# Mixture of experts: a chunk's preparation given out piece by piece beside the first experts, and a second bank for the gates

## The chip, the cores and the metric

One core of one Trainium2 chip runs the kernel. The time is device microseconds of one execution. Lower is better. Six names are used for what works in parallel: PE is TensorE's matmul, PEld its weight load, DVE is VectorE, ACT is ScalarE, POOL is GpSimd, and SP is SyncE, which here only issues transfers.

## The reference

An activation `x` of 2048 tokens of 128 numbers goes through a chain of attention and feed-forward layers, each added to `x`. Five kinds of layer are used (the small linear Ffn0, Moe1, Mamba, Moe2, and Attn2, Attn3, Ffn3 at the end); the change is about the two mixtures of experts. Each of the two is applied twice:

```
x = x + 0.5 * _L1_ffn_ref(_layernorm(x, axis=-1), ...)      # Moe1
x = x + _L1_attn_ref(_layernorm(x, axis=-1), ...)           # Mamba
x = x + 0.5 * _L1_ffn_ref(_layernorm(x, axis=-1), ...)      # Moe1
x = x + 0.5 * _L2_ffn_ref(_layernorm(x, axis=-1), ...)      # Moe2
x = x + _L2_attn_ref(_layernorm(x, axis=-1), ...)           # Attn2
x = x + 0.5 * _L2_ffn_ref(_layernorm(x, axis=-1), ...)      # Moe2
```

Moe1 picks 2 of 16 experts for each token, and adds a shared expert:

```
logits = flat @ router_w.T
topk_scores, topk_idx = jax.lax.top_k(logits + router_bias, TOPK)
topk_scores = jax.nn.softmax(topk_scores, axis=-1)
combine = combine.at[jnp.arange(N)[:, None], topk_idx].add(topk_scores)
hidden = jax.nn.silu(gate_all) * up_all
down_all = jnp.einsum('nke,ked->nkd', hidden, down_proj)
out = jnp.einsum('nk,nkd->nd', combine, down_all)
sh_hidden = jax.nn.silu(flat @ sh_gate.T) * (flat @ sh_up.T)
```

Moe2 picks 4 of 16 experts. Each expert has a hidden layer of 256:

```
combine = jnp.sum(jax.nn.one_hot(topi, E, dtype=...) * topw[..., None], axis=2)
hmid = jax.nn.gelu(x @ w1e + b1e, approximate=False)
return (acc + (hmid @ w2e + b2e) * ce[:, None], None)
```

Both are computed densely: every expert works on every token, and the combination weight (zero for experts not picked) is multiplied in.

## The kernel before

`x` stays on the chip, transposed: 128 features on the partitions, 2048 tokens along the free axis. A stage (one layer) works on four chunks of 512 tokens. All matmuls of the experts are written three times, with the operands split into a high and a low half (`mm3`: high by high, high by low, low by high).

**An expert.** In Moe1 (`main`, L576) the main loop makes 9 steps: eight pairs of experts (each of hidden size 64, two side by side on 128 partitions) and the shared expert. A step computes gates `g` and ups `u` into PSUM, then `y = silu(g)` on ACT, `u = y * u` and `z = u * c` on DVE (the product with the combination weights), splits `z` into `yh` (ACT) and `yl` (POOL), and accumulates `o`. In the text a step of Moe1 is also called an expert. In Moe2 (`main`, L682) there are 16 experts of two half steps each: `h` into PSUM (four banks in turn), Gelu on ACT, the product with `c` on DVE (`h<-h,c` or `y<-h,c`, so 32 products in a chunk), the split (its low half on DVE or POOL), and `o`.

**The weights of the experts.** `c` is a tile with the combination weights of two steps, broadcast to all partitions. It comes by a transfer on SP from the DRAM tile `rows` (`group`, L518, transfer at L524); group 0 of a chunk serves the first two steps, group 1 the next two, and so on. Main asks for the next group at each even step. The pool of `c` has three buffers (`room`, L529), handed out in the order of the program.

**The preparation of a chunk.** It is a Python generator (`steps`) that the main loop of the chunk ahead of it is woven with, and it has five pieces: (1) the layer norm (`centred`, squares, a power on POOL, transposes), (2) the split of the normed tokens and the router's matmul to logits, (3) the choice of the top 2 or 4 with DVE reductions (`combine`, L446), (4) the softmax weights and the `comb` matrix, (5) its transposes on PE, the copy `row` on ACT, the transfer `rows<-row` on SP (L514), and behind it the transfer of the chunk's first group (`rows`, L507). That first group of the next chunk is called N0 below: in the program it stands between two groups of the chunk that is being worked on.

**The order.** `weave` (L328) drives the main generator; after its i-th step it gives out pieces of the other generator as long as the count `at` satisfies the line below. Other work joins in: splits of the next stage's weights and pieces of the next stage's own preparation (`joined`, `early`), each of which raises the total `prep` by its number.

```python
while not done and at * self.MAIN < i * prep:
```

`MAIN` is the number of steps, `PREP` the number that stands for the stage's own preparation, and `EARLY` how many pieces of the stage behind are taken in early. With MAIN, PREP of 9, 7 the five pieces come after steps 1, 2, 3, 4 and 6; with 16, 7 after steps 1, 3, 5, 7 and 10. Where other work joins, the places shift. A scheduler then orders each engine's instructions: the program's order is the priority, and an instruction of later pieces may be put ahead if it is thought ready earlier. The order on each engine is fixed when the kernel is built.

**PSUM.** It has eight banks of 128 x 512 floats. In Moe1 they are: two shared ones for preparation (`pp`), two lent in addition (`lend`, L266), one for `o`, one for `g`, two for `u`. In Moe2: two shared, one lent, one `o`, four `h`. `pt` hands out the shared and lent banks in turn.

**The last stage step of Attn2** (`run`, L1789) gives Moe2's weight splits and its first chunk's preparation beside its last block, with the total `after.PREP + k`, where k is the 16 splits.

Of the kernel before, what the change touches and what calls it, by code (L numbers as in the profile page):

```python
# [29 lines left out]
P = 128  # L30
NT = 2048
SEQ = 256
NB = 8
CH = 512
# [213 lines left out]
class Stage:  # L248
# [3 lines left out]
    EARLY = (0, 0)  # L252
# [27 lines left out]
    def enter(self):  # L280
        pass
# [4 lines left out]
    def run(self, st, then):  # L286
        for c in range(NCH):
            if c == NCH - 3:
                with self.m.behind():
                    after, gen = then()  # L290
            if c == NCH - 1:
                return self.weave(self.main(c, st), (after, gen))
            own, n, rest = self.steps(c + 1), 0, self.m.rest
            if c == NCH - 2 and after and after.todo:
                own, n = self.joined(own, after.splits(), len(after.todo))
                own, k = self.joined(own, gen, after.EARLY[1])
                st = self.weave(self.main(c, st), (self, own), self.PREP + n + k)
                continue
            if rest:
                own, n = self.joined(own, *rest)  # L300
            if c >= NCH - 3 and after:

                own, n = self.joined(own, gen, after.EARLY[c - NCH + 3])
            st = self.weave(self.main(c, st), (self, own), self.PREP + n)
            if rest:
                self.m.rest = self.m.under.close()
# [21 lines left out]
    def weave(self, main, ahead, prep=None):  # L328

        stage, gen = ahead  # L330
        res, done, at = None, gen is None, 0
        prep = prep or (stage.PREP if stage else 0)
        for i, _ in enumerate(main, 1):
            while not done and at * self.MAIN < i * prep:
                try:
                    next(gen)
                    at += 1
                except StopIteration as e:
                    res, done = e.value, True
        return res if done else stage.finish(gen)  # L340
# [36 lines left out]
class Ffn0(Stage):  # L377


    PIECES = 3  # L380
# [32 lines left out]
class Moe(Stage):  # L413

    RAW, LAG = 7, 2

    def split(self, w, src, share):


        n = src.shape[-1]  # L420
        self.raw = ExitStack()
        tp = self.m.tc.tile_pool(name="raw", bufs=self.RAW, side=self.side, reuse_waits="tile")
        self.todo = []
        pool = self.raw.enter_context(tp)
        for at in range(0, n, CH):
            k = slice(at, min(n, at + CH))
            lower = self.nc.gpsimd if at // CH % share < share - 1 else None
            self.todo.append((pool, w[0][:, k], w[1][:, k], src[:, k], lower))
        self.raws = [self.fetch(*x) for x in self.todo[: self.RAW]]
# [109 lines left out]
class Moe1(Moe):  # L539


    MAIN, PREP, EARLY = 9, 7, (1, 3)
    SIDE = 2

    def open(self, side):
# [24 lines left out]

    def enter(self):
        self.ps = self.pool("m1p", 1, late=True, space=PSUM)
        self.lend(2)
        self.yk = self.pool("m1y", 3, late=True)

    def main(self, c, st):  # L576
        m, ps, yk = self.m, self.ps, self.yk
        hh, hl, ct = st
        rows, cg = ct if ct[1] else self.given
        h = (hh[:], hl[:])  # L580

        part = lambda i, k: [w[:, (3 * k + i) * P : (3 * k + i + 1) * P] for w in self.w]
        op = self.t(ps, [P, CH], "o")
        for k in range(9):
            if k % 2 == 0 and k < 8:

                cs, cg = cg, k < 6 and self.group(rows, k // 2 + 1)
            g = self.t(ps, [P, CH], "g")
            m.mm3(g[:], part(1, k), h)
            u = self.t(ps, [P, CH], "u", bufs=2)  # L590
            m.mm3(u[:], part(0, k), h)
            y = self.t(yk, [P, CH], "y")
            m.act(y[:], g[:], AF.Silu)
            z = self.t(yk, [P, CH], "z")
            if k < 8:
                m.tt(u[:], y[:], u[:], ALU.mult)
                m.tt(z[:], u[:], cs[:, k % 2, :], ALU.mult)
            else:
                m.tt(z[:], y[:], u[:], ALU.mult)
            yh = self.t(yk, [P, CH], "yh", dtype=F32R)  # L600
            yl = self.t(yk, [P, CH], "yl", dtype=F32R)
            m.halves(yh[:], yl[:], z[:], self.nc.gpsimd)
            m.mm3(op[:], part(2, k), (yh[:], yl[:]), k == 0, k == 8)
            if k < 8:
                yield
        m.stt(m.x(c), op[:], 0.5, m.x(c), ALU.mult, ALU.add)
        yield


class Moe2(Moe):  # L610


    MAIN, PREP, EARLY = 16, 7, (0, 3)
    SIDE = 1

    def open(self, side):
# [179 lines left out]
class Attn0(Stage):  # L796


    MAIN, PREP = 17, 12
# [224 lines left out]
class Mamba(Stage):  # L1024


    MAIN, PREP, EARLY = 16, 26, (2, 10)
# [457 lines left out]
    def beside(self, main, gens):  # L1485

        for i, _ in enumerate(main):
            for k in self.PLAN[i]:
                if k in gens:
                    next(gens[k], None)  # L1490
            yield
        for gen in gens.values():
            for _ in gen:
                pass
# [48 lines left out]
class Attn2(Stage):  # L1543


    MAIN, PREP = 11, 30
# [232 lines left out]
    ps = None  # L1779
# [9 lines left out]
    def run(self, st, then):  # L1789
        ready, half = st  # L1790
        for s in range(NB - 2):
            ahead = self, self.mix(self.stack(s + 1, half), self.project(s + 2))
            ready, half = self.weave(self.main(s, ready), ahead)
        after, gen = then(False)
        n = after.EARLY[1] if after else 0
        main = self.main(NB - 2, ready)
        st = self.weave(main, (self, self.early(self.stack(NB - 1, half), gen, n)), 19 + n)
        self.more.close()
        if after is None:
            return self.weave(self.main(NB - 1, st), (after, gen))  # L1800
        after.load()
        k = len(after.todo)
        gen = self.early(gen, after.splits(), k)
        return self.weave(self.main(NB - 1, st), (after, gen), after.PREP + k)

    def main(self, s, st):
        m, nc, wk, ps = self.m, self.nc, self.mk, self.ps
# [61 lines left out]
class Attn3(Stage):  # L1869


    MAIN, PREP, EARLY = 5, 8, (4, 8)
# [468 lines left out]
```

## Time and profile before

| what | us |
|---|---|
| median of 3 runs | 2684.03 |
| the runs | 2673.51, 2684.03, 5309.02 |
| the profiled execution | 2682.87 |
| its span in the profile | 2681.1 |

The page's second part gives each engine's busy share in 40 slices of the span, in tenths, and the clock that was granted to TensorE:

```profile
PE   6999998978888998898986898997988799789997
DVE  3666555459999899999998667877876776457653
PEclk7999998989999899899887998999998899799998
```

A slice is 67 us. The first Moe1 lies in the 7th to 9th (411 to 551 us), Mamba behind it up to the 22nd, then the second Moe1 and the first Moe2 (1465 to 1809 us), Attn2, and the second Moe2 (2036 to 2277 us). In Mamba DVE and POOL set the pace, in the mixtures PE does. The page's fourth part follows the chain of work that ended last:

```profile
PE 44%; DVE 18%; DMA 11%; ACT 10%; POOL 7%; issue 6%; SPq 4%; DVEq 0%; ACTq 0%; POOLq 0%
```

Seen chunk by chunk, the windows in which the four chunks were worked on lasted 35, 32, 28 and 44 us in the first Moe1, 53 (with a load of weights at its start), 19, 30 and 15 in the second, 71, 54, 47 and 55 in the first Moe2, and 71, 70, 54 and 46 in the second.

Waits are read like this: `A <- B: 6.7, 8, 1.8` says that instructions of kind A waited for B for 6.7 us in all, 8 times, 1.8 us the longest. In a timeline the idle time ahead of an instruction stands in brackets at its end, with what ended it.

### The profile page before, as it was taken

What the parts mean: (1) busy time and instruction counts of PE and PEld (TensorE: products, weight loads), DVE (VectorE), ACT (ScalarE), POOL (GpSimd) and SP (SyncE); (2) the same over time, 40 slices, a digit from 0 to 9 for tenths busy, and PEclk for the clock granted to TensorE, in tenths of its full rate; (3) what the DMA queues carried; (4) which work ended last, traced back from release to release, by engine and by line L of the source; (5) the groups of instructions that cost most, each with busy time, mean ns of one, the idle gap of its engine ahead of it and who ended that gap; (6) DMA issues with size and microseconds to landing.
All of it is one profiled execution on the core that took longest, in us unless ns stands there. A gap on an engine that the chain in (4) does not pass through costs nothing.

```text
span 2681.1 us, 36786 instructions
## 1 busy us (share of the span) xinstructions
PE 2348.9 (88%) x11655; PEld 1463.9 (55%) x11655; DVE 1950.2 (73%) x3164; ACT 1884.1 (70%) x4390; POOL 1639.1 (61%) x1223
## 2 busy tenths in 40 slices
PE   6999998978888998898986898997988799789997
PEld 5777766643333333333322666776766677556655
DVE  3666555459999899999998667877876776457653
ACT  5877876677777777777654666784556687678875
POOL 2555555459999999999997854551125455434531
PEclk7999998989999899899887998999998899799998
DMA  6656653233443344333442442322223221244430
GB/s 167 136 129 142 142 122 99 66 89 88 115 94 79 84 91 114 80 81 76 93 101 61 117 122 97 103 68 64 67 68 108 83 78 58 60 82 91 96 60 9
DMA packets 136338, 246.53 MB, mean 92 GB/s; under 512 B 17008, under 2 KB 60976, under 8 KB 136144
## 3 DMA queue, kind: packets, MB, share of 16 engines
q1 hardware_dynamic: 134640, 240.45, 36.4%
q10 hardware_dynamic: 1248, 3.48, 0.6%
q8 instruction: 93, 1.52, 0.2%
q14 instruction: 101, 0.83, 0.1%
q0 software_dynamic: 256, 0.25, 0.0%
HBM read 138.11 MB, written 21.50 MB: 60 GB/s over the span
## 4 chain that ended last, share of the span: by engine, by line
PE 44%; DVE 18%; DMA 11%; ACT 10%; POOL 7%; issue 6%; SPq 4%; DVEq 0%; ACTq 0%; POOLq 0%
PE pp L135 12%; DVE hs L1344 8%; PE o L135 6%; PE h L135 5%; PE sp L135 4%; POOL hs L1350 4%; DVE up L143 4%; PE op L135 3%; DMA du<-du 3%; PE u L135 3%; PE ss L135 2%; PE y L135 2%; PE tp L999 2%; DMA c<-rows 2%; DMA kl<-kl 1%
## 5 line engine op out<-in xcount | busy, mean ns | idle before, releaser
L1350 POOL TENSOR_TENSOR hs<-hs,cl 128x1024 f32<-128x1024 f32 x256 | 602.5, 2372 | 67.2 <-DVE hs L1344 47.7
L1344 DVE TENSOR_TENSOR_SCAN hs<-dA,up 128x1024 f32<-128x1024 f32 x192 | 439.0, 2286 | 22.9
L135 PE MATMUL y<-hs,ysel 128*64 128x512 f32 x1024 | 302.5, 672 | 46.5 <-POOL hs L1350 44.4
L993 POOL TENSOR_SCALAR pr<-pr,sums 128x256 f32<-128x256 f32 x192 | 175.4, 924 | 187.1 <-DVE sums L988 171.1
L167 ACT ACTIVATE dA<-dt,negA 128x510 f32<-128x510 f32 x384 | 251.4, 713 | 5.8 <-DVE hs L1344 4.5
L143 DVE TENSOR_TENSOR up<-up,du 128x1024 f32<-128x1024 f32 x192 | 233.3, 1215 | 29.7 <-PE up L135 21.9
L167 ACT ACTIVATE h<-h,vec 128x512 f32<-128x512 f32 x256 | 168.1, 667 | 60.1 <-PE h L135 56.0
L227 POOL TENSOR_TENSOR ln_r<-ln_r,mhalf 128x2 f32<-128x2 f32 (+2 forms) x116 | 90.3, 779 | 185.2 <-ACT ln_r L167 183.6
L135 PE MATMUL pp<-xp,w_hi 128*128 128x512 f32 x320 | 139.9, 520 | 23.5 <-ACT pre L167 23.5
L201 POOL TENSOR_TENSOR yl<-y,yh 128x512 fp32r<-128x512 f32 x64 | 83.9, 1311 | 114.7 <-ACT yh L167 113.7
L1304 POOL TENSOR_TENSOR hs<-du,bl 128x1024 f32<-128x1024 f32 x64 | 151.8, 2372 | 0.0
L1344 DVE TENSOR_TENSOR_SCAN hs<-up,hs 128x1024 f32<-128x1024 f32 x64 | 145.1, 2268 | 2.9 <-POOL hs L1304 2.4
L135 PE MATMUL o<-yl,wh 128*128 128x512 f32 x328 | 137.2, 418 | 6.3 <-POOL yl L201 5.2
L135 PEld LDWEIGHTS y<-hs,ysel 128*64 128x64 f32 x1024 | 53.8, 143 | 162.7 <-POOL hs L1350 77.5
L201 POOL TENSOR_TENSOR yl<-z,yh 128x512 fp32r<-128x512 f32 x72 | 92.2, 1285 | 80.0 <-ACT yh L167 78.9
L135 PE MATMUL o<-yh,wh 128*128 128x512 f32 x328 | 135.2, 412 | 4.3 <-ACT yh L167 4.3
L167 ACT ACTIVATE pr<-sp,nmax 128x256 f32<-128x256 f32 x256 | 120.8, 483 | 23.2 <-DVE nmax L980 10.1
L135 PE MATMUL h<-hh,wh 128*128 128x512 f32 x256 | 107.3, 419 | 30.2 <-DVE y L143 29.1
L143 DVE TENSOR_TENSOR h<-h,c 128x512 f32<-128x512 f32 x128 | 89.0, 696 | 61.4 <-ACT h L167 40.1
L135 PE MATMUL up<-bp,bsel 128*128 128x512 f32 x192 | 101.8, 531 | 36.1 <-DVE hs L1344 31.7
L135 PE MATMUL o<-yh,wl 128*128 128x512 f32 x328 | 130.8, 399 | 0.0
L167 ACT ACTIVATE ln_q<-pp 128x128 f32<-128x128 f32 x348 | 97.0, 279 | 46.9 <-PE pp L135 38.9
(417 smaller groups left out, 6917.1 us busy)
## 6 DMA issues: line engine op xcount, KB each, us to landing
c<-rows SPq DMA_DIRECT2D x64, 512.0 KB
cl<-states SPq DMA_DIRECT2D x62, 512.0 KB
c<-rows SPq DMA_DIRECT2D x64, 256.0 KB
dt<-dt SPq DMA_DIRECT2D x128, 128.0 KB
du<-du SPq DMA_DIRECT2D x128, 128.0 KB
k<-kh SPq DMA_DIRECT2D x60, 256.0 KB
kl<-kl SPq DMA_DIRECT2D x60, 256.0 KB
scr<-hi SPq DMA_DIRECT2D x96, 128.0 KB
```

What stands on the lines that cost most here:

```text
L135: return self.pin(self.nc.tensor.matmul(out, lhsT, rhs, start=start, stop=stop))
L143: return self.pin(self.nc.vector.tensor_tensor(out, in0, in1, op))
L167: i = self.nc.scalar.activation(out, in_, func, **kw)
L201: i = (lower or self.nc.vector).tensor_tensor(lo, x, hi, ALU.subtract)
L227: self.nc.gpsimd.tensor_tensor(out, out, self.mhalf[:, 0 : out.shape[-1]], ALU.pow)
L993: nc.gpsimd.tensor_scalar(pr[:, t, :], pr[:, t, :], sums[:, t : t + 1], None, ALU.mult)
L999: nc.tensor.transpose(tp[:, j, t, :], pr[:, t, j * P : (j + 1) * P], m.ident[:])
L1304: self.m.pin(self.nc.gpsimd.tensor_tensor(self.hs[g][:], du[:], b, ALU.mult))
L1344: m.pin(nc.vector.tensor_tensor_scan(x[:].rearrange("p g t -> p (g t)"), self.decays.pop(g).rearrange("p g b t -> p (g b t)"), u[:].rearra ...
L1350: m.pin(nc.gpsimd.tensor_tensor(x[:], x[:], c, ALU.mult))
```

## The change

Four numbers change, and a name is added:

```diff
 class Moe(Stage):
     RAW, LAG = 7, 2
+    PIECES = 5
...
 class Moe1(Moe):
-    MAIN, PREP, EARLY = 9, 7, (1, 3)
+    MAIN, PREP, EARLY = 9, 9, (1, 3)
...
     def enter(self):
         self.ps = self.pool("m1p", 1, late=True, space=PSUM)
-        self.lend(2)
+        self.lend(1)
...
-            g = self.t(ps, [P, CH], "g")
+            g = self.t(ps, [P, CH], "g", bufs=2)
...
 class Moe2(Moe):
-    MAIN, PREP, EARLY = 16, 7, (0, 3)
+    MAIN, PREP, EARLY = 16, 16, (0, 3)
...
 Attn2.run
-        return self.weave(self.main(NB - 1, st), (after, gen), after.PREP + k)
+        return self.weave(self.main(NB - 1, st), (after, gen), after.PIECES + k)
```

With PREP equal to MAIN the five pieces come after steps 1, 2, 3, 4 and 5, one after each, in Moe1 as in Moe2. Where other work joins, the fifth piece comes after these steps (before, after): first Moe1, chunk 0: 7, 6; chunk 1: 7, 5; chunk 2: 5, 4; second Moe1, chunks 0 and 1: 6, 5; chunk 2: 4, 4; first Moe2, chunks 0 to 2: 10, 5; second Moe2: 10, 5; 12, 7; 9, 6. The last chunk of a stage takes the number of the stage behind it. In Moe1 the gates get a second PSUM bank, and preparation loses one of its four. In Attn2's last block the total is 21 where it was 23.

## The prediction

> **What bounds the kernel now.** I read the page's first part first, then the busy time of each engine in four stretches: the first Moe1 stage (411 to 551), the second Moe1 with the first Moe2 (1465 to 1582, 1582 to 1809) and the second Moe2 (2036 to 2277). They are 725 us of the 2681.1 us span; the change touches little else. Columns: the stretch, its length, then busy us of PE, PEld, DVE, ACT, POOL with instruction counts, granted PE clock, DMA share, GB/s.
>
> ```profile
> PE 2348.9 (88%) x11655; PEld 1463.9 (55%) x11655; DVE 1950.2 (73%) x3164; ACT 1884.1 (70%) x4390; POOL 1639.1 (61%) x1223
> ...
> 411.00:551.00 140.00, 126.73 (x518) 91.44 (x519) 67.98 (x152) 94.41 (x221) 73.10 (x64) 0.91 0.25 61
> 1465.00:1582.00 117.00, 98.39 (x424) 74.78 (x425) 71.71 (x186) 70.29 (x160) 80.44 (x66) 0.94 0.49 134
> 1582.00:1809.00 227.00, 210.58 (x939) 167.38 (x938) 172.52 (x379) 176.30 (x328) 120.08 (x120) 0.96 0.29 93
> 2036.00:2277.00 241.00, 218.07 (x980) 171.95 (x979) 171.97 (x365) 174.99 (x393) 123.07 (x112) 0.96 0.23 76
> ```
>
> PE is the busiest everywhere, idle 13.3, 18.6, 16.4 and 22.9 us: 71 us in all is the most that can be won, and 18.6 of it holds a load of weights. So I asked the second Moe2 who waits, and looked at the longest wait on SP, DVE and PE. First SP's timeline: start, us, queue, line, transfer, count.
>
> ```profile
> 2047.55 10.98 SPq L524 DMA_DIRECT2D c<-rows  x3
> 2081.91 0.32 SPq L514 DMA_DIRECT2D rows<-row  x1
> 2083.89 21.43 SPq L524 DMA_DIRECT2D c<-rows  x6
> ```
>
> ```profile
> SPq L514 <- ACT row L167: 57.6, 3, 23.4
> ```
>
> Then DVE and PE over the same microseconds.
>
> ```profile
> 2077.23 0.22 DVE L143 TENSOR_TENSOR comb<-comb,pp 128x64 f32<-128x64 f32 x1
> ...
> 2090.46 0.70 DVE L143 TENSOR_TENSOR h<-h,c 128x512 f32<-128x512 f32 x1 [10.51 <-DMA c<-rows]
> ```
>
> ```profile
> 2080.95 0.39 PE L135 MATMUL o<-yh,wl 128*128 128x512 f32 x1
> 2091.81 0.80 PE L135 MATMUL h<-hh,wh 128*128 128x512 f32 x1 [10.47 <-DVE y L143]
> 2092.40 0.63 PE L135 MATMUL h<-hl,wh 128*128 128x512 f32 x1
> ```
>
> The next chunk's selection ends (2077.45), its transposes and ACT copy follow, and `rows<-row` goes out at 2081.91, SP having waited 23.4 us for the copy. Only behind it come the next chunk's first group (N0) **and this chunk's own groups 6 and 7**: 24 products had been done (12 experts, groups 0 to 5), and product 25 waits until 2090.46. From `rows<-row` to that product it is 8.6 us, in the first Moe2 9.0 (1621.77 to 1630.73). So place on SP is what costs: whatever stands behind N0 waits for the whole preparation. The first Moe2 does the same, PE gap 8.1 us; chunk 1 of the second has a 5.5 us wait on DVE after product 28 and a PE gap of 3.4.
>
> What the rows wait for is a chain, not a place. First centred tile to rows: 1583.1 to 1621.8 = 39 us (first Moe2), 2038.4 to 2081.9 = 43 us (second). In the former the logits come near expert 6 though placed beside the third, the selection at 1599 to 1611, the combination at 1616 to 1619. In chunks 1 and 2 of the first Moe2 rows leave after 5 and 2 of the chunk's 32 products, ahead of a place beside expert 10: placement isn't binding there either.
>
> **The change, part by part.** All against the profiled execution, 2682.87 us (span 2681.1 plus 1.8), 1.2 under the median 2684.03; the runs spread from 2673.5.
>
> *Second bank for g.* No instruction is added. In Moe1's two stretches PE waits for its single bank:
>
> ```profile
> PE g L135 <- ACT y L167: 6.7, 8, 1.8
> PE u L135 <- DVE z L143: 5.8, 5, 2.6
> ```
>
> and 2.2 us in the first: 8.9 together. Next late is u's bank, freed by DVE: 5.8 and 3.5 us already. I give half of 8.9: **−4** (−8.9 to 0). A row of the skill speaks lower, in the page "TensorE: Matmul & The Clock Gate", section "HAM oscillation — how this bites in real kernels": in its thin-M kernel a double-buffered PSUM brought nothing further (126.6 to 125.5 us). By it this term would be nearly 0 and the sum 4 higher; no run here shows which.
>
> *One bank less for preparation* (lent 2 to 1, so 4 to 3 with the shared pair). Moe2 runs its preparation and the guests' projections on 3 already. In Moe1 the guests are Ffn0, Mamba and the weight splits. **+2**: near 0 since Moe2 lives with it; at most 8, some 16 Mamba and Ffn0 pieces at half a microsecond (the `pp` matmul's mean, 520 ns).
>
> *Pieces earlier in Moe1* (PREP 7 to 9): fifth piece from beside expert 6 or 7 to 5 or 4. Each piece carries its ACT, PE and POOL work, one `rows<-row` and two N0 transfers on SP. Two stalls of Moe1 lie behind rows: PE gaps of 1.6 (476.8) and 2.6 us (1556.7). Chains of 22 to 30 us fill most of a 19 to 35 us chunk whatever the place: **−1** (−4.2 to 0). In the first Moe1's chunk 2 N0 now also passes the own group 3: three experts more stand behind rows that came after its 9th product. **+1** (0 to 6.3: three experts at 19/9 = 2.1 us, from the second Moe1's shortest chunk); Mamba's pieces fill that hole (PE 28.0 of 28 us busy there now).
>
> *Moe2, PREP 7 to 16*: piece 5 moves from beside expert 10 to 5. SP takes N0 in program order, so groups 4 and 5 go behind it: what is ahead covers 8 experts, not 12. An undisturbed chunk (1707 to 1754, PE 46.94 of 47 us busy) is 47/16 = 2.93 us an expert: the cover loses 4 × 2.93 = 11.7 us. For it, DVE, on which the chain waits, is relieved of the four experts' work while the rows are being made: per expert two products (0.70 and 0.69) and an `yl` (0.68) = 2.07 us, together 8.3. Net 11.7 − 8.3 = +3.4 for each chunk where own groups now wait, with the clock's part below +4. If ACT or POOL and not DVE holds the chain, all 11.7 is paid; if precedence shortens it by more, the present stall (10.5) goes: −11 to +11.7, and I take the value near DVE because the combination's dozen DVE operations stand right behind products 23 and 24. First Moe2 chunk 0: **+4**. Second, chunk 0: **+4**, chunk 1 (place 12 to 7): **+3.4** (−3.4 to 11.7), chunk 2 (9 to 6): **+3** (0 to 11.7): its rows come when 10 experts are done, 12 being covered now and 8 then; 2 × 2.93 = 5.9 are missing, of which Attn3's pieces (PE 53.9 of 54 us there) fill half. First Moe2 chunks 1 and 2: rows are early, N0 only holds one of three c buffers longer. Two suffice: from 1704 on N0 held one, groups went out every 5.6 to 6.3 us, one lands in 3.7: 0.
>
> The clock: after gaps of 8.1 and 10.5 us matmuls start 0.43 us apart instead of 0.23, 12 and 8 of them: 2.4 and 1.6 us, already paid. The same page, section "What's actually happening", has an idle window of about 3.4 us halving the clock and as much busy time restoring it; the rows agree. By it a longer gap costs nothing more, a new one some 1.7 (an estimate).
>
> *Attn2's count* (7 + 16 to 5 + 16): pieces of its last block shift by one main step; **0** (−3 to 3, POOL's longest wait there is 4.4).
>
> *Next Moe2's pieces beside Moe1's last chunk* (PREP of the guest): 4 and 5 a step sooner, 0.
>
> Sum: −4 + 2 − 1 + 1 + 4 + 4 + 3.4 + 3 = **+12.4**, 2695 us.
>
> **The rivals.**
>
> R0, slower: the chain isn't relieved. It is latency over POOL's powers, PE's transposes and ACT, which the moved products don't touch. Then four Moe2 chunks pay 11.7 and Moe1 6.3, with the bank's 2: 46.8 + 6.3 + 2 = +55, **2738**. For it: the same 46 us for chunk 3's chain (1654 to 1700), which ran with nothing placed before it. It decides if the second Moe2's first chain still takes 43 us from the first centred tile to rows.
>
> R1, faster: the pieces move forward and rows with them. Gaps of 8.1 + 10.5 + 3.4 go, the slow clock's 4.0, the whole g 8.9 and Moe1's 4.2: −39.5, **2643**; at half of that 2663. For it: Moe1's chains are 22 to 30 us, and an early priority could give Moe2 the same; 8 experts cover 23 us. Against: the logits were three experts behind their place.
>
> R2, nothing: SP's order by readiness lets the groups pass N0, as in the first Moe2's chunks 1 and 2, and the bank is covered: **2683**. Against: 23.4 us of SP waiting in front of ready groups.
>
> **How the numbers follow.** Two per cent, 54 us, is about what a measurement here tells from no change: faster below 2630, slower above 2738. Forecast 0.50 (its own range 2683 to 2715), R0 0.15, R1 0.22, R2 0.13. The range leaves out the upper half of R0 and the lower third of R1: 2655 to 2738. R0 stands at the bound, so half of it, 0.08, and 0.04 of the forecast's tail are slower: 0.12. Of R1 0.04 is below 2630, if Moe1's holes go too. The rest, 0.84, is the same.
>
> **What would show it.** In the second Moe2's chunk 0, `rows<-row` with 16 products before it, not 24, and then a DVE wait for `c<-rows` at product 17 with a PE gap of 12 to 15 us behind it; the same in the first. That chain at 35 us instead of 43 shows the relief; 43 shows R0; 25 or less R1. In Moe1 `g <- ACT y` gone from PE's waits and `u <- DVE z` above 9.3 shows the bank's half. A wait of PE for a `pp` bank in Mamba's pieces would show the lent bank's price. It is wrong altogether if groups 4 and 5 go out ahead of rows.

## The result, and the profile after

The changed kernel takes 2712.4 us (median of 4 runs, 2705 to 2716) where the kernel before took 2678.8 beside it: a ratio of 1.0131, 95% interval [1.0089, 1.0173]. One execution of the kernel before took 5309 us; it is in its median, but not in the ratio, which compares fast runs alone. A later comparison on another chip gave 1.0097 [1.0070, 1.0124]. The change makes the kernel slower, clearly more than by chance, and by less than 2%. The forecast was 2695 with 2655 to 2738. Below, a gain or loss of a run in us is its ratio put on the time of the kernel before, so 35 and 26 us here.

The profiled execution has a span of 2703.4 us. These are its windows of the same stretches, cut at its own stage ends (the columns are those of before: stretch, length, busy us of PE, PEld, DVE, ACT and POOL, clock, DMA share, GB/s):

```profile
411.00:541.00 130.00, 116.66 (x513) 87.76 (x511) 68.18 (x149) 90.99 (x209) 71.18 (x62) 0.96 0.25 61
1463.00:1583.00 120.00, 99.98 (x429) 77.03 (x429) 74.84 (x181) 73.76 (x174) 81.69 (x68) 0.89 0.49 128
1583.00:1805.00 222.00, 207.67 (x910) 162.78 (x908) 167.69 (x370) 174.77 (x313) 119.40 (x119) 0.98 0.29 95
2040.50:2293.70 253.20, 224.86 (x971) 176.08 (x970) 169.39 (x364) 173.93 (x378) 122.76 (x111) 0.92 0.22 72
```

The first Moe2 (third line) is 222 us long instead of 227, the second 253 instead of 241, and PE has 28 us there in which it does nothing, and a granted clock of 0.92 instead of 0.96. The same microseconds as before, at the first rows of the second Moe2, on SP:

```profile
2052.08 0.33 SPq L525 DMA_DIRECT2D c<-rows  x1
2077.74 0.33 SPq L515 DMA_DIRECT2D rows<-row  x1
2079.36 33.68 SPq L525 DMA_DIRECT2D c<-rows  x8
```

on DVE:

```profile
2074.92 0.22 DVE L143 TENSOR_TENSOR comb<-comb,pp 128x64 f32<-128x64 f32 x1
...
2085.74 0.70 DVE L143 TENSOR_TENSOR h<-h,c 128x512 f32<-128x512 f32 x1 [9.97 <-DMA c<-rows]
```

and on PE:

```profile
2076.54 0.39 PE L135 MATMUL o<-yh,wl 128*128 128x512 f32 x1
2087.09 0.80 PE L135 MATMUL h<-hh,wh 128*128 128x512 f32 x1 [10.16 <-DVE y L143]
2087.68 0.63 PE L135 MATMUL h<-hl,wh 128*128 128x512 f32 x1
```

Before `rows<-row` only one group (group 3) goes out where three did; then SP issues nothing for 25 us. DVE has done 16 of the chunk's products, idles 9.97 us and PE 10.16 us. The third chunk, in which DVE had no wait for `c` before, has one now:

```profile
2218.48 0.70 DVE L143 TENSOR_TENSOR h<-h,c 128x512 f32<-128x512 f32 x1 [8.92 <-DMA c<-rows]
```

It is again product 17 of its chunk. Over the second Moe2, SP's wait for the copy grew from 57.6 to 83.1 us (three waits each):

```profile
SPq L515 <- ACT row L167: 83.1, 3, 34.1
```

Lengths of the stages by profile, in us, from the last addition to `x` of one stage to that of the next. Names with e_ are the experiments; two names in one row are two profiles of one kernel.

| kernel | Moe1 | Mamba | Moe1 | Moe2 | Attn2 | Moe2 | behind it |
|---|---|---|---|---|---|---|---|
| before | 141.7 | 916.9 | 115.9 | 226.8 | 227.3 | 240.4 | 404.6 |
| changed | 134.9 | 921.7 | 120.6 | 221.7 | 235.7 | 253.2 | 409.6 |
| changed, second profile (e_after) | 137.2 | 921.2 | 120.0 | 221.6 | 235.1 | 255.5 | 408.9 |
| e_a2: Attn2's total alone | 138.9 | 918.4 | 118.2 | 226.9 | 232.1 | 240.7 | 403.4 |
| e_bank: the banks alone | 136.1 | 921.5 | 121.4 | 214.4 | 232.7 | 234.1 | 414.1 |
| e_m1, e_m1again: Moe1's places alone | 141.7, 141.8 | 922.1, 914.1 | 120.1, 117.1 | 229.3, 229.3 | 231.4, 229.2 | 240.6, 240.8 | 415.2, 413.3 |
| e_m2: Moe2's places alone | 139.4 | 922.2 | 123.5 | 230.7 | 226.6 | 252.9 | 412.5 |
| e_mid: changed, N0 after step 10 | 134.9 | 925.0 | 118.6 | 216.0 | 234.8 | 234.1 | 412.0 |
| e_late: changed, N0 after step 13 | 136.9 | 928.2 | 119.4 | 211.2 | 230.9 | 220.9 | 416.2 |
| e_best: before, banks, Moe2's places, N0 after step 13 | 136.0 | 919.0 | 119.2 | 212.1 | 231.6 | 222.5 | 424.4 |
| e_late7: e_late, Moe1's places as before | 135.0 | 926.7 | 121.2 | 212.1 | 235.1 | 222.9 | 425.3 |
| e_bankm1: the banks and Moe1's places | 139.8 | 923.0 | 119.2 | 217.4 | 232.2 | 234.7 | 410.7 |
| e_jit: before, another order | 141.5 | 923.9 | 118.2 | 228.0 | 226.7 | 237.0 | 419.8 |

Before and e_a2 have the same program up to Attn2's last block, and nearly the same behind it. Their rows show what chance does: 3 us in the first Moe1, but 0.1 and 0.3 in the two Moe2. e_m2 has before's program up to the second Moe1, where Moe2's first pieces join, and its Mamba is 5 us longer: that too is chance. The two profiles of e_m1 differ by 8 us in Mamba and by 0.0 and 0.2 in Moe2. So the Moe2 columns can be read to a microsecond or two, Mamba's can't.

### The profile page after: what moved, and what is told of

Same layout as the page of the kernel before. It is cut to its first block, busy times and chain, and to the rows that moved or that the text cites. A ratio compares the mean times of both kernels' runs of the same rounds, so it can differ in the third digit from the quotient of the medians.

```text
span 2703.4 us, 36801 instructions
## 1 busy us (share of the span) xinstructions
PE 2351.0 (87%) x11655; PEld 1468.7 (54%) x11655; DVE 1959.1 (72%) x3164; ACT 1889.6 (70%) x4390; POOL 1640.3 (61%) x1223
## 4 chain that ended last, share of the span: by engine, by line
PE 35%; DVE 18%; DMA 8%; POOL 8%; ACT 8%; issue 5%; SPq 3%; DVEq 0%; POOLq 0%; ACTq 0%
PE pp L135 8%; DVE hs L1345 7%; PE o L135 7%; PE h L135 6%; POOL hs L1351 4%; DVE up L143 3%; PE u L135 3%; DMA du<-du 3%; PE sp L135 2%; PE ss L135 2%; PE y L135 1%; DMA c<-rows 1%; PE g L135 1%; POOL hs L1305 1%; PE acc L135 1%
## 5 line engine op out<-in xcount | busy, mean ns | idle before, releaser
L135 PE MATMUL o<-yl,wh 128*128 128x512 f32 x328 | 136.9, 418 | 9.0 <-POOL yl L201 4.4
L201 POOL TENSOR_TENSOR yl<-z,yh 128x512 fp32r<-128x512 f32 x72 | 91.7, 1287 | 67.9 <-ACT yh L167 62.5
L981 DVE TENSOR_REDUCE nmax<-sp 128x2 f32<-128x512 f32 x128 | 87.5, 687 | 57.2 <-PE sp L135 55.7
```

The costliest lines, as they stand in the source:

```text
L135: return self.pin(self.nc.tensor.matmul(out, lhsT, rhs, start=start, stop=stop))
L201: i = (lower or self.nc.vector).tensor_tensor(lo, x, hi, ALU.subtract)
L981: nc.vector.tensor_reduce(nmax[:], sp[:], AX.X, ALU.max, negate=True)
```

## The experiments

Theory T: the loss lies in Moe2, where own groups now stand behind N0, and so behind a preparation that can't be finished in time. Rivals: the bank that preparation lost, the places in Moe1, the count in Attn2, or the early pieces themselves. The first four runs do one part alone.

**The banks alone** (e_bank):

```diff
-        self.lend(2)
+        self.lend(1)
...
-            g = self.t(ps, [P, CH], "g")
+            g = self.t(ps, [P, CH], "g", bufs=2)
```

> Only the gates' second bank and the smaller loan (lend 1), every place as before. Theory (the loss comes from the places in Moe2; the bank helps Moe1): the waits of g for ACT's y (2.2 and 6.7 us) go, the first Moe1 gets 4 to 9 us shorter, Moe2 is unchanged, in all -4 (-9 to 0) against before. Rival (the lent bank is missed): PE waits for a pp bank beside Mamba's and Ffn0's pieces, 0 to +8 in all.

2678.8 against 2683.3 us, ratio 0.9973 [0.9949, 0.9996]: 7 us faster, as expected in size. The first Moe1 is 5.6 us shorter, as expected too; over all profiles it took 134.9 to 139.8 us with the banks (8 profiles) and 138.9 to 141.8 without (6). But the waits that were to go are not the reason: PE's waits in the first Moe1 still have one of 6.1 us for `y`,

```profile
PE g L135 <- ACT y L167: 7.4, 2, 6.1
PE u L135 <- DVE z L143: 4.8, 5, 1.2
```

and the two Moe2, which have no edit of it, got shorter as well, by 12.4 and 6.3 us. Their first rows leave 32.1 us (39.8 before) and 40.5 us (45.9) after the stage's start. The order on the engines is another, and the traces show which step moved: in all eight profiles with the banks the layer norm of Moe2's chunk 1 starts 25 to 37 us ahead of the stage (its first `pp<-cmat,xT` on PE), in all six without them 1 to 3 us behind its start. The first `comb` instruction of chunk 1 then stands behind product 17 of the first Moe2 on DVE, not 23, and behind 19 of the second, not 24. Why an edit of Moe1's banks moves that layer norm wasn't settled. Two candidates are the phase in which `pt` hands out its banks and the readiness that the scheduler assumes; neither was tried.

**Moe1's places alone** (e_m1, twice):

```diff
-    MAIN, PREP, EARLY = 9, 7, (1, 3)
+    MAIN, PREP, EARLY = 9, 9, (1, 3)
```

> Only Moe1's PREP 9, banks and Moe2 as before. Theory: the first Moe1's chunk 2 gets the wait of 13 us on DVE for the group that is behind rows (in the changed kernel at product 25), PE partly covered by Mamba's pieces: 0 to +6 in all. Rival (places in Moe1 bring what the changed kernel won there): the first Moe1 6 to 7 us shorter.

> Moe1's PREP 9 alone once more, unchanged, for its size and for a second profile. Theory (the 17 are real and in one place): +10 to +23 again, and the same stage longer in both profiles. Rival (the first comparison was high by chance of the chip or the runs): +5 or less.

1.0065 [1.0043, 1.0087] and, on another chip, 1.0069 [1.0047, 1.0090]: 17 and 18 us slower. The wait that was expected is there, as long as expected (the first Moe1's waits, first profile):

```profile
DVE z L143 <- DMA c<-rows: 15.9, 2, 13.8
```

but it costs nothing there: chunk 2 lasts 42.7 us instead of 28.5, chunk 3 30.5 instead of 43.4, since PE does 22 matmuls more in the former and 22 less in the latter, and the stage is 141.7 us long as before. What is longer in both profiles is the first Moe2 (2.5 us) and, with 9 to 11 us most of all, the stretch behind the second Moe2, where no edit is. Its middle, 140 us from 120 us behind the second Moe2 on, first of before and then of e_m1:

```profile
2396.40:2536.40 140.00, 133.52 (x859) 92.12 (x858) 100.06 (x244) 120.43 (x322) 67.30 (x57) 0.98 0.41 86
```

```profile
2413.40:2553.40 140.00, 126.52 (x778) 87.46 (x777) 90.12 (x226) 107.98 (x285) 54.23 (x47) 0.91 0.42 84
```

PE does 81 instructions less there and has a lower clock (0.91; in the second profile 66 less and 0.93). The part alone is slower, by its own comparison; that the cost comes from another order behind the second Moe2 is what two profiles of one column say, and no run isolates it.

**Moe2's places alone** (e_m2; Attn2's total stays 23):

```diff
-    MAIN, PREP, EARLY = 16, 7, (0, 3)
+    MAIN, PREP, EARLY = 16, 16, (0, 3)
```

> Only Moe2's PREP 16; Attn2's last block keeps its total of 23, Moe1 as before. Theory: the first Moe2 5 us shorter (rows 10 us earlier), the second 10 to 13 us longer (waits for c at products 17 of chunks 0 and 2, at product 21 of chunk 1), behind it some us more: +8 to +20, most of the change's loss. Rival (the loss is the bank's or Attn2's): within 5 us of before.

2715.9 against 2683.3 us, ratio 1.0111 [1.0074, 1.0149], 30 us: as much as the whole change, and more than the 8 to 20 expected. The second Moe2 is 252.9 us long, 12.5 more. The first is not shorter but 3.9 us longer: what the changed kernel won there came with the banks. So the two Moe2 hold 16.4 of the 30; the rest lies, by one profile, in stages that this edit doesn't touch or hardly touches (the second Moe1 7.6 us longer, the stretch behind the second Moe2 7.9). This run differs from the kernel before in Moe2's places only, and shows chunk by chunk what they do: the chunks of the second Moe2 last 9.0 and 5.3 us longer and 0.4 and 1.6 shorter. DVE waits for `c` at product 17 of chunk 0 and at product 21 of chunk 1:

```profile
DVE h L143 <- DMA c<-rows: 18.7, 2, 10.6
```

In chunk 2 the rows left after 11 products, and there is no such wait.

**Attn2's total alone** (e_a2):

```diff
-        return self.weave(self.main(NB - 1, st), (after, gen), after.PREP + k)
+        return self.weave(self.main(NB - 1, st), (after, gen), 5 + k)
```

> Only Attn2's total, 5 + 16 = 21 instead of 23. Theory: nothing, within 3 us of before. Rival (the 8 us that Attn2 lasts longer in the changed kernel come from its count): Attn2 4 to 9 us longer.

1.0002 [0.9985, 1.0020]: nothing, within 4 us less and 5 more, and the order of the instructions is nearly the same. Attn2 itself is 4.8 us longer in the one profile, which is what the rival said; but with the count of 23 it took 226.6 to 232.7 us, so this run can't tell.

**N0 moved back** (e_late, e_mid). These keep the changed kernel's early places for the first four pieces, the transposes and the ACT copy, and move only the two transfers:

```diff
-        return hh, hl, self.spread(comb[:], c)
+        got = self.spread(comb[:], c)
+        for _ in range(8 if c else 0):
+            yield
+        return hh, hl, (got[0], *self.send(got[1]))
```

In e_mid the 8 is a 5. `spread` now ends with the copy to `row`; `send`, which is not shown, issues `rows<-row` and N0.

> The changed kernel, but in Moe2 the two transfers of the fifth piece (rows and the next chunk's first group N0) are given out 8 steps later, after step 13, behind all own groups; the other pieces stay beside experts 1 to 5. Theory (Moe2's loss is own groups held behind N0): no DVE wait for c in the middle of a chunk, the second Moe2 225 to 235 us (253 in the changed kernel, 240 before), the first 212 to 220; in all 15 to 30 faster than the changed kernel, so -5 to +20 against before. Rival (the early pieces themselves take DVE, ACT and PE from the experts): the second Moe2 stays at 248 to 255.

> As the run before, with 5 steps instead of 8: N0 stands where the kernel before had it (behind step 10, groups 0 to 5 in front), while the pieces run early. Theory: rows come some 8 to 10 us earlier in the chunk than before and 12 experts cover them, so the waits of both kernels are nearly gone: the second Moe2 228 to 238. Rival (the chain isn't shortened by the early places, only by the DVE idling behind product 16): rows as late as before, 43 us from the first centred tile, and a wait of 8 to 10 us at product 25, the second Moe2 240 or more.

e_late: 2670.5 against 2684.9 us, ratio 0.9938 [0.9916, 0.9961], 17 us faster than before and, by the ratios, some 40 to 50 faster than the changed kernel, which was not run beside it. SP and DVE at the first rows of its second Moe2:

```profile
2045.89 23.04 SPq L536 DMA_DIRECT2D c<-rows  x5
2075.55 0.32 SPq L526 DMA_DIRECT2D rows<-row  x1
2077.16 15.66 SPq L536 DMA_DIRECT2D c<-rows  x4
```

```profile
2074.55 0.68 DVE L201 TENSOR_TENSOR yl<-h,yh 128x512 fp32r<-128x512 f32 x1
2076.76 0.70 DVE L143 TENSOR_TENSOR h<-h,c 128x512 f32<-128x512 f32 x1 [1.53 <-ACT h L167]
```

All five own groups, 3 to 7, go out before rows, and product 25 waits 1.5 us for ACT and for no transfer. SP's wait for the copy is down to 26.9 us. The two Moe2, in windows:

```profile
1593.00:1804.20 211.20, 203.35 (x909) 160.04 (x908) 167.11 (x370) 172.83 (x313) 118.82 (x119) 1.00 0.31 100
2035.10:2256.00 220.90, 212.26 (x971) 168.46 (x971) 167.89 (x365) 170.49 (x378) 122.91 (x111) 0.99 0.25 83
```

PE is idle 7.9 and 8.6 us, and the clock is 1.00 and 0.99. The second Moe2 lost 32 us of its 253, more than expected, and the rival (early pieces take the engines from the experts) falls.

e_mid: 2680.7 against 2684.9 us, 0.9979 [0.9962, 0.9997]. Here the second Moe2 is as long as expected, but not for the reason given. Rows leave 32.1 and 41.0 us after the stage's start, as late as with the banks alone (32.1 and 40.5), where the pieces stood at their old places, and the chunks last as long too: 59.8, 52.1, 46.9 in the first Moe2 against 59.5, 52.1, 46.9. In both kernels the rows go out as soon as the copy is done, so it is the chain that is late. Giving the pieces out early brings nothing; the place of N0 is what counts. The second Moe2 by that place (of chunk 0): 253.2 us after step 5, 234.1 after step 10, 220.9 after step 13.

**Combinations.** e_best is the kernel before with the banks, Moe2's early places and N0 late; Moe1's PREP stays 7. e_late7 is e_late with Moe1's PREP 7; it differs from e_best in Attn2's total only. e_bankm1 has the banks and Moe1's PREP 9.

> The kernel before with the gates' second bank, and Moe2's pieces early with rows and N0 after step 13; Moe1's PREP 7 as before. Theory: the bank's -7 and 10 to 15 us from the second Moe2, 5 to 10 from the first: -15 to -35 against before, faster than either kernel. Rival (the order of the tail or of the first Moe2 gives it back): within 7 of the run with the bank alone.

> The changed kernel with rows and N0 late in Moe2 (e_late), and Moe1's PREP back to 7. Theory (PREP 9 costs in Moe1, where N0 passes group 3 of the first Moe1's chunk 2): 5 to 15 faster than e_late, some -20 to -30 against before. Rival (it costs nothing beside the second bank): within 5 of e_late, -10 to -20.

> The gates' second bank and Moe1's PREP 9 together, Moe2 and Attn2 as before. Theory (the +17 of PREP 9 alone come from the one bank of g and the wait behind rows in Moe1, and go with the second bank): as the bank alone, -7 (-12 to -2) against before. Rival (PREP 9 costs its 17 whatever the banks are): +5 to +15.

e_best 0.9963 [0.9938, 0.9987], e_late7 0.9970 [0.9948, 0.9993], e_bankm1 0.9991 [0.9972, 1.0010]. The two Moe2 are 212.1 and 222.5 us in e_best, 212.1 and 222.9 in e_late7: as in e_late. In all, e_best and e_late7 were expected 5 to 25 us faster than they are, e_bankm1 lies between its two theories. What the first two won there is, by one profile each, given back behind the second Moe2, which took 424 and 425 us (405 before). PREP 9 beside the second bank (e_bankm1 against e_bank) costs some 5 us, with overlapping intervals; beside e_late it costs nothing. So the 17 us of Moe1's places are no constant that can be added.

e_bankm1 also isolates the loss of the change. It differs from the changed kernel only in Moe2's places and Attn2's total, which alone does nothing, and both stood beside the same runs of the kernel before: 0.9991 against 1.0097, a step of some 28 us. Between the profiles of e_bankm1 and of e_after the two Moe2 grow by 4.2 and 20.8 us, all the rest together shrinks by 4. Over the second Moe2, DVE's waits for `c`, first of e_bankm1 and then of e_after:

```profile
DVE h L143 <- DMA c<-rows: 9.2, 2, 4.7
```

```profile
DVE h L143 <- DMA c<-rows: 20.6, 3, 10.0
```

**Order without work** (e_jit). If the order behind the second Moe2 costs, it should do so when nothing else is changed:

```diff
+            if self.tight and c == 0 and e == 0:
+                for _ in range(20):
+                    m.nc.vector.memset(self.jit[:], 0.0)
```

> The kernel before with 20 memsets of 128x16 on DVE (some 1.2 us of DVE by the 60 ns of such a memset in the trace) that nothing waits for, in Attn2; they change no place and no bank, but the scheduler then orders 200 instructions of DVE in the second Moe2 and 600 behind it otherwise. Theory (part of what all edits cost is the order behind Moe2, 404 us long before and 410 to 415 in all the kernels with another order): 3 to 12 us slower than before, behind the second Moe2. Rival (that length is chance from run to run): within 2 us of before.

2683.9 against 2684.9 us, 1.0011 [0.9989, 1.0032]. The memsets ran at 1765 to 1771 us, in the first Moe2 and not in Attn2, since nothing holds them back. The one profile is 15 us longer behind the second Moe2, but its execution, 2703 us, was the slowest of twelve that went from 2675 to 2703. This changed order costs nothing that shows, so the length of that stretch in one profile is weak evidence; the interval, 3 us less to 9 more, leaves room for the lower part of the theory's 3 to 12.

**The changed kernel again** (e_after):

> The changed kernel once more, on one chip with e_late7, for a second profile of it. Theory (the second Moe2's 253 us and its waits at products 17 are fixed by the order): 250 to 256 again, +25 to +40 against before; Mamba and what lies behind the second Moe2 differ by several us from its first profile. Rival (the stages vary by chance as much as the change moves them): the second Moe2 below 247.

1.0097 [1.0070, 1.0124], 26 us; the second Moe2 255.5 us, 2.3 above the first profile, Attn2 0.6 below. It answers to the theory.

## Why the prediction was right, and where its steps were off

The direction, the mechanism and the range held; the size was 12 where 35 and 26 were measured. The step that was mis-sized is Moe2's places: +14.4 in the sum (+4 and +10.4), where they cost 16.4 us in the two Moe2 alone (e_m2) and 25.0 beside the banks (e_after against e_bankm1). That the total stayed well inside the range is in part luck: the banks' 19 us in the two Moe2, which the sum did not have, stand against it. Without them the total would be some 45 to 54 us (an estimate from these numbers), near the upper bound of 2738.

- **Own groups behind N0 in Moe2**: shown. With 16 products in front instead of 24, DVE and PE wait at product 17 of chunks 0 and 2, and putting N0 behind the own groups takes those waits away, and 32 us of the second Moe2.
- **The net of +4 for each first chunk**: the relief was mis-sized. 8.3 us of DVE work were to come off the chain. Rows do leave 8.7 us earlier in the second Moe2 (37.2 against 45.9 us), which looks like a hit, but 4.9 of it come with the banks (41.0 in e_mid, where N0 is at its old place); only 3.8 are relief, and in the first Moe2 3.9 (28.2 against 32.1). 11.7 of cover less 3.8 of relief is +7.9. Measured against e_mid: chunk 0 went from 59.8 to 67.9 us and from 67.6 to 76.2, +8.1 and +8.6. e_m2 against before, without any banks, says the same: the rows leave 3.4 and 4.0 us earlier, and chunk 0 lasts 6.6 and 9.0 us longer. The sign set for the relief, the second Moe2's chain from the first centred tile to rows, reads 39.1 us there: between the 43 of R0 and the 35 of full relief. In the changed kernel it can't be read, because that tile is made 32 us ahead of the stage. The 0.6 that makes 3.4 a 4 was given to the clock and worked out from no row.
- **By chunk of the second Moe2, against before**: +5.1, +0.7, +8.2, −1.4 (forecast +4, +3.4, +3, none); in e_m2 +9.0, +5.3, −0.4, −1.6. The term of chunk 2 fits neither kernel: in the changed one Attn3's pieces don't fill its hole (PE 56.8 of 62.1 us; 11.0 us longer than in e_mid), and in e_m2, where the rows left after 11 products and not 16, there is no hole. In the changed kernel's chunk 1 product 21 does come 7.0 us after the rows, but the chunk of before had a wait of 5.5 us too.
- **First Moe2**: forecast +4; alone +3.9, in the changed kernel −5.1, since the banks' −12.4 lies in the same stage. That an edit of Moe1 would move Moe2's layer norm ahead was no term of the sum. The 3.7 us that a group takes to land is in no row; the traffic of the one issued at 1704.21 was over some 3 us later.
- **g's second bank and the lost one** (−4 and +2): −7 together. The waits that were to vanish are partly there: 2.2 to 1.2 us in the first Moe1, 6.7 to 5.9 in the second of the changed kernel. Half of the step's reason fails: the first Moe1 is some 4 us shorter with the banks, more than the 2.2 us that PE waited for g there, the second Moe1 is not shorter, and the two Moe2 gained 19 us that were no part of the reason. The Trainium skill's example, a double-buffered PSUM that brings nothing further ("TensorE: Matmul & The Clock Gate", section "HAM oscillation — how this bites in real kernels"), is not borne out in the total of −7, and is nearer to what g's own waits show. No run here has the second bank without the lost one.
- **Moe1's places** (−1 and +1): right for the stage, whose hole of 13.8 us Mamba's pieces did fill; alone the part costs 17 us, beside the second bank some 5, which the sum had nowhere.
- **Attn2** (0): right for the total (1.0002 alone). The 4.4 us given as POOL's longest wait is in the trace as a wait of PE for POOL; POOL itself waited 6.1 us in that block.
- **Clock**: a longer gap was to cost nothing more, a new one some. After the changed kernel's PE gap of 10.16 us matmuls start 0.43 us apart for 6.1 us; after the 10.47 and 8.12 us of before they did for 3.4 and 5.7. So gaps of about the same length don't cost the same, and of the busy time of about 3.4 us, with which the prediction says that the rows agree, only one of these three is an instance. The changed kernel's second Moe2 was granted 0.92 where e_late, without such gaps, had 0.99.
- **R0** (the chain isn't relieved, 2738) was nearer than the forecast for the first chunks: 8 us of 11.7 were paid. **R1** and **R2** fall. (R1's gains add up to 39.1, not 39.5.)

What stays open: why Moe1's places cost 17 us without the second bank and some 5 with it, why the banks move Moe2's layer norm, and why the stretch behind the second Moe2, which no edit touches, is 4 to 21 us longer in every kernel but e_a2.

## What to carry to other kernels

Where a transfer that waits for a long chain shares an in-order queue with transfers that the running loop needs, its place in that queue matters more than when its chain starts: put it behind the last one that the loop needs. Here that one move turned a change of some +30 us into −17. A static order that a scheduler builds answers to edits in stages far away, so the gains and losses of parts measured alone needn't add up: −7, +17, +30 and 0 make 40, and 35 and 26 were measured. Taking parts back out of the whole (e_bankm1) showed where the loss lies more plainly than putting them in one at a time.

## What was not expected

A bank in Moe1 shortened the first Moe2 by some 12 us (226.8 to 214.4, and beside Moe1's places 229.3 to 217.4), through an order that is fixed when the kernel is built: the next chunk's layer norm runs before the stage begins. And stages differ in how well they repeat: Moe2 to 0.3 us between two profiles of one program (2.3 at the most), Mamba by 8.
